# Cross-attention in seven products: other signs, a denominator taken from T3, and a new order around half 1

## The chip, the cores and the metric

The kernel runs on one NeuronCore of a Trainium2 chip. The metric is the device time of one execution in microseconds (us); lower is better. Engines are named as in the profile: PE (TensorE matmul), PEld (its weight loads), DVE (VectorE), ACT (ScalarE), POOL (GpSimd), SP (SyncE, which here only issues DMAs).

## What is computed

```python
q = jnp.einsum('bcn,dc->bnd', x1, Wq) + bq
k = jnp.einsum('bcn,dc->bdn', x2, Wk) + bk[:, None]
v = jnp.einsum('bcn,dc->bdn', x2, Wv) + bv[:, None]
attn = jax.nn.softmax(jnp.einsum('bnd,bdm->bnm', q, k), axis=2)
return jnp.einsum('bcm,bnm->bcn', v, attn) + x1
```

All is float32. There are 8 batches (b0 to b7 below), C = 512 channels, D = 64, N = 1024 positions. The softmax runs over m (the keys).

## The kernel before

**Two big products per batch.** The kernel first forms Y = x2 · softmax' (512 x 1024 by 1024 x 1024, the softmax without its denominator) and then out = Wv · Y + bv + x1. Each of the two is cut into quarters "11", "12", "21", "22" and done with seven products instead of eight (Winograd's form), numbered 1, 2, 6, 7, 5, 3, 4 in the order in which a table (MULT, L408) and the code run them. A product takes a left sum (of x2's quarters: S1 to S4) and a right sum (of the exponentials' quarters: T1 to T4). "y1" below is product 1 of Y, "o6" is product 6 of out.

In the exponentials, h is the half of the queries n (tile e[h]) and g the half of the keys m. The quarters are named in open_t: "11" is e[0] at g 0, "21" is e[0] at g 1, "12" is e[1] at g 0, "22" is e[1] at g 1. So "12" and "22" together are all of query half 1, and their sum over m is that half's denominator. Before the change the sums are T1 = 12 - 11, T2 = T1 - 22, T3 = 22 - 12 (written over "12"), T4 = 21 + T2; and S1 = 21 + 22, S2 = 11 - S1, S3 = 11 - 21, S4 = 12 + S2.

**A product inside a product.** Most Y products (multiply_seeded, L595) are once more cut into quarters and done by seven small products of 128 x 256 (inner_product, L513; four matmul records each). Their own left sums (left_stream, L478, four DVE operations of 128x256) and right sums (right_stream, L491, one DVE operation of 128x1024 and two of 128x512) are called "left" and "right" of a product below; the tiles are eI1, eI2, eI5, eI7, eI3, eI4 (right) and aI (left). Inside one product ACT copies the chain bank four times and one bank to an SBUF tile v; complete (L624) lets DVE add v at the end. A dictionary of hooks puts further ACT work between these steps.

**Order.** The program is written out by hand (manual_schedule), each engine runs its instructions in the order of the code, and waits are put between engines where tiles depend on each other. A tile with one buffer under a tag is only written again once its last reader is done, a DMA that stores it included. period (L868) is one batch: y1, y2, y6, the scores of the next batch n for half 0 (and the queries of the one after, nn), y5, y7, y3, scores of n for half 1 (and keys of nn), y4, then o1, o6, o2, o5 and o7 woven, o3, o4. b0 has its own branch; b1 to b5 have n and nn (the code's `five`); b6 has no nn; b7 has neither.

**What the change touches.**

- Softmax of a half: fold (L242) and fold_halves (L256) make a running maximum or sum over key tiles on DVE, highest (L260) and total (L266) end it with an all-reduce over partitions on POOL (L264, L269). Then invert (L275) takes the reciprocal and writes a row to DRAM, spread (L281) reads it back over 128 partitions; shares is both. lower (L296) subtracts the maximum on DVE, exponential (L306) is ACT's exp. Half 0's sum is made by accumulating DMAs (add_tile, L723).
- Denominator of half 1: three folds of e[1] on DVE, at the start of the batch's own period, and total(s, 1).
- T sums: sum_e (L349) is T1 and T2 on DVE. sum_t3 (L338) negates "12" on ACT and adds "22" by an accumulating DMA that POOL issues. copy_t4 (ACT) and add_t4 (POOL's DMA) make T4.
- S1 of the next batch: begin_s1 (L152) loads a quarter by SP, end_s1 (L157) adds another by POOL's DMA; negate and add_11 make S2 and S3 from it.
- Results: evict_o (L670) takes a quarter of out from PSUM; for "11", "22" and "12" POOL's DMA adds x1 and SP stores the tile (L720, L721). The tile of "11" has the tag u1, that of "12" the tag r. u1 is also a tile of product 5's right sums, r is also the tile v of product 5.
- PSUM banks: the scores' second tile (b1 to b5) or third (b6) goes to bank "c", which evict_y(s, "11") reads before.

```python
            weave(folds(s, 1, "sum", ALU.add), left_stream(s, 7, s.a["S3"], "yT4"))
            total(s, 1)
            invert(s, 0)
            complete_2 = multiply_seeded(
                s, 2, "y22", {5: lambda: copy_u1(s, 0), 4: lambda: copy_u1(s, 1)}
            )
            sum_t3(s, 0)
            sum_t3(s, 2)
            complete_2()
            evict_y(s, "11")
            copy_t4(s)
            add_t4(s)
```

Of the kernel before, what the change touches and what calls it, by code (L numbers as in the profile page):

```python
# [15 lines left out]
def kernel(  # L16
# [84 lines left out]
    def left_sums(a, *ks):  # L101

        for k in ks:
            if k == "S3":
                nc.vector.tensor_tensor(a["21"], a["11"], a["21"], ALU.subtract)
                a["S3"] = a["21"]
            elif k == "S4":
                nc.vector.tensor_tensor(a[k], a["12"], a["S2"], ALU.add)
            else:
                x, y, op = {"S1": ("21", "22", ALU.add), "S2": ("11", "S1", ALU.subtract)}[k]  # L110
                nc.vector.tensor_tensor(a[k], a[x], a[y], op)
# [13 lines left out]
    class Batch:  # L125
        def __init__(self, b):
            self.b = b
            self.a, self.e, self.t, self.y, self.o = {}, {}, {}, {}, {}
            self.mx, self.top, self.den, self.few, self.rden, self.row = {}, {}, {}, {}, {}, {}
            self.tmp, self.bank = {}, {}  # L130
            self.inner = {}

# [18 lines left out]

    def begin_s1(s):  # L152
# [113 lines left out]
    def total(s, h):  # L266
        fold_halves(s, h, ALU.add)
        s.den[h] = sb.tile([P, H], F32, tag="den", name=f"den_{s.b}_{h}", bufs=2)
# [45 lines left out]
    def right_sums(t, k):  # L314

        x, y = {"T1": ("12", "11"), "T2": ("T1", "22"), "T3": ("22", "12"), "T4": ("21", "T2")}[k]
        nc.vector.tensor_tensor(t[k], t[x], t[y], ALU.add if k == "T4" else ALU.subtract)
# [8 lines left out]
    def copy_t4(s):  # L326

        s.t["T4"] = t4 = sb.tile([P, MH, H], F32, tag="eT4", name=f"eT4_{s.b}")
        for i in (0, 2):
            nc.scalar.copy(t4[:, i : i + 2, :], s.t["21"][:, i : i + 2, :])  # L330
# [7 lines left out]
    def sum_t3(s, i):  # L338

        t3 = s.t["T3"][:, i : i + 2, :]  # L340
        nc.scalar.mul(t3, t3, -1.0)
        nc.gpsimd.dma_start(t3, s.t["22"][:, i : i + 2, :], accum_op=ALU.add)

    def copy_u1(s, j):
        if j == 0:
            s.tmp[1] = sb.tile([P, 2, H], F32, tag="yT1", name=f"uy1_{s.b}")
        nc.scalar.copy(s.tmp[1][:, j, :], s.bank["a", j])
# [51 lines left out]

    def iter_t4(s):  # L400
        sum_y(s, "T4")
        yield
# [126 lines left out]
    def inner_parts(s, i):  # L529

        ks = ("third", "chain") if i in (2, 7) else ("chain", "third")
        of = {k: ps_s.tile([P, 2, H], F32, tag="sc", name=f"ps_i{i}{k}_{s.b}")[:, 0, left] for k in ks}
        return of["chain"], of["third"]
# [61 lines left out]
    def multiply_seeded(s, i, v_tag, hooks={}, bank=None):  # L595
# [11 lines left out]
        v = sb.tile([P, 2, H], F32, tag=v_tag, name=f"v{i}_{s.b}")[:, 0, left]  # L607
# [16 lines left out]
        def complete():  # L624
            b = b1.rearrange("p (a n) -> p a n", a=2)
            nc.vector.tensor_tensor(b, b, v.unsqueeze(1).to_broadcast([P, 2, H // 2]), ALU.add)
# [6 lines left out]
    def copy_7(s, j):  # L633
        if j == 0:
            s.tmp[7] = sb.tile([P, 2, H], F32, tag="u1", name=f"uy7_{s.b}")
        nc.scalar.copy(s.tmp[7][:, j, :], s.bank["c", j])
# [15 lines left out]
    def evict_y(s, k):  # L652

        bank, add = RESULT[k]
        if k == "22" or s.b == B - 1 and k == "21":
            bank, add = "a", 6
        s.y[k] = y = sb.tile([P, 2, H], F32, tag=f"y{k}", name=f"y{k}_{s.b}")
        for j in range(2):
            nc.vector.tensor_tensor(y[:, j, :], s.bank[bank, j], s.tmp[add][:, j, :], ALU.add)
# [10 lines left out]
    def evict_o(s, k):  # L670
# [37 lines left out]
        if add is None:  # L708
            o = sb.tile([P, 2, H], F32, tag="u1" if k == "11" else "r", name=f"r{k}_{s.b}")
            for j in range(2):  # L710
                nc.scalar.activation(o[:, j, :], s.bank[bank, j], AF.Identity, bias=bias(j))  # L711
        else:
# [6 lines left out]
        if k != "21":  # L719
            nc.gpsimd.dma_start(o, block(s, k, x1), accum_op=ALU.add)  # L720
        nc.sync.dma_start(block(s, k, out), o)  # L721
# [146 lines left out]
    def period(s, n, nn, nnn):  # L868
# [25 lines left out]
        def scores_0():  # L894
            then = scores_and(n, 0, 1 if nn else 2, "c", next_queries if nn else nothing)
            if nn is None:
                first(6, (1,))
            if s.b:
                for i in range(1, MH):
                    fold(n, 0, i, "max", ALU.max)  # L900
                highest(n, 0)
            return then
# [4 lines left out]

        def first_sum():
# [3 lines left out]
        open_t(s)  # L912
        if s.b == 0:
# [6 lines left out]
            s.a["S4"] = sb.tile([P, MH, C // 2], F32, tag="aS4", name=f"aS4_{s.b}")  # L920
            nc.scalar.copy(s.a["S4"], s.a["S2"])
            nc.gpsimd.dma_start(s.a["S4"], x2T[s.b, 0, 1], accum_op=ALU.add)
# [12 lines left out]
            for i in range(1, MH):  # L935
# [29 lines left out]
        else:  # L965
            complete_1 = multiply_seeded(s, 1, "y11")
            sum_e(s, "T1", "T2")
            complete_1()
            sums_5 = left_stream(s, 5, s.a["S1"], "i2"), right_stream(s, 5, s.t["T1"], "y21", "u1")
            if n:  # L970
                weave(folds(s, 1, "sum", ALU.add), left_stream(s, 7, s.a["S3"], "yT4"))
                total(s, 1)
                invert(s, 0)
            else:
                weave(folds(s, 1, "sum", ALU.add), left_stream(s, 7, s.a["S3"], "yT4"))
                weave(*sums_5)
            complete_2 = multiply_seeded(
                s, 2, "y22", {5: lambda: copy_u1(s, 0), 4: lambda: copy_u1(s, 1)}
            )
            sum_t3(s, 0)  # L980
            sum_t3(s, 2)
            if n is None:
                total(s, 1)
            complete_2()
            evict_y(s, "11")
            copy_t4(s)
            add_t4(s)
            first(6, (0,) if n and nn is None else range(2))
            if n:
                weave(*sums_5)  # L990
            if n:
                sum_a(s, "S4")
                evict_q = scores_0()
                spread(s, 0)
                shares(s, 1)
            if n:
                weave(right_stream(s, 7, s.t["T3"], "yT1", "yT2"), left_stream(s, 3, s.a["S4"], "aI3"))
            else:
                sum_a(s, "S4")
                weave(right_stream(s, 7, s.t["T3"], "yT1", "yT2"), left_stream(s, 3, s.a["S4"], "aI3"))  # L1000
                invert(s, 0)
                spread(s, 0)
# [4 lines left out]
            if n is None:  # L1007
                shares(s, 1)
            if n:
                weave(right_stream(s, 3, s.t["22"], "eT1"), lowers(n, 0, 0, 1))  # L1010
# [8 lines left out]
            if n:  # L1019
                lower(n, 0, 1)  # L1020
            complete_3 = multiply_seeded(s, 3, "r", hooks, "c")
# [6 lines left out]
            if n:  # L1028
                for i in range(2, MH):
                    lower(n, 0, i)  # L1030
            complete_3()
            evict_t3(s)
        if n:
            if s.b:
                load_a(n, "11")
            begin_s1(n)
# [15 lines left out]
            end_s1(n)  # L1052
            if nn:
                next_keys()
        if late and n:
            weave(left_stream(s, 4, s.a["22"], "a12"), right_stream(s, 4, s.t["T4"], "eT2"))
        if late:
            scale_y(s, "11", "T3", "22")
# [3 lines left out]
        if five:  # L1062
            weave(folds(n, 1, "max", ALU.max))
# [8 lines left out]
        if five:  # L1072
            highest(n, 1)
        complete_4()
        if late and n:
            negate(n, "S3")
# [10 lines left out]
        scale_y(s, "21")  # L1087
        if s.b == 0:
# [4 lines left out]
        if five:  # L1093
            weave(iter_t4(s), right_stream(s, "o7", s.y["T3"], "eT1"))
# [4 lines left out]
        if late and n and not five:  # L1099
            weave(folds(n, 1, "max", ALU.max), right_stream(s, "o7", s.y["T3"], "eT1"))  # L1100
# [11 lines left out]
        second(6)  # L1112
        if n:
# [8 lines left out]
        evict_o(s, "11")  # L1122
        if n:
            if not five:
                add_tile(n, 0, 3)
            if late:
                inner_left(n, 1, n.a["11"], "i2")
        if late:
            complete_7, rest = multiply_57(s)
        else:  # L1130
# [4 lines left out]
        if n:  # L1135
            for i in range(MH) if s.b else (2,):
# [5 lines left out]
        if n:  # L1142
            negate(n, "S2")
            add_11(n, "S2")
        evict_o(s, "22")
# [3 lines left out]
        if n:  # L1149
            weave(  # L1150
                right_stream(n, 1, n.e[0][:, 0], "yT1", "yT2"), left_stream(n, 2, n.a["12"], "aS4")
# [4 lines left out]
            evict_o(s, "12")  # L1156
# [46 lines left out]
```

## Time and profile before

| what | value |
|---|---|
| median of 3 runs | 677.41 us (676.89 to 677.58) |
| the profiled execution's own time | 677.15 us |
| its span in the profile | 675.4 us |
| granted TensorE clock, mean | 0.998 |
| moved by DMA | 134.26 MB, 199 GB/s |

The span runs from the first to the last instruction of the program in the profile; 1.75 us of the execution lie around it. A row of the timeline gives start, duration, engine, line, operation and tiles, how many instructions of the kind follow each other (x4), and in brackets how long the engine idled before it and what ended that. A matmul on PE is pipelined: its record's duration is longer than the step from one to the next, so steps are read from the starts.

### The profile page before, as it was taken

How to read it: one execution, taken by the hardware profiler on the slowest of the kernel's cores; microseconds unless marked ns; L12 is line 12 of the kernel's file. 1: busy time of each engine (PE TensorE's matmuls, PEld its weight loads, DVE VectorE, ACT ScalarE, POOL GpSimd, SP SyncE). 2: the span in 40 equal slices, each digit the busy share in tenths (PEclk: the TensorE clock that was granted, in tenths of full speed). 3: DMA queues.
4: the chain of work that ended last, by engine and by line, in shares of the span. 5: the costliest groups of instructions: out<-in, count | busy, mean ns of one | idle time of the engine just before them, and what ended most of it. 6: DMA issues, size and time to landing. Idle time of an engine off the chain costs nothing.

```text
span 675.4 us, 7565 instructions
## 1 busy us (share of the span) xinstructions
PE 666.4 (99%) x2510; PEld 413.1 (61%) x2510; DVE 612.5 (91%) x811; ACT 358.5 (53%) x619; POOL 218.2 (32%) x188
## 2 busy tenths in 40 slices
PE   8999999999999999999999999999999999999996
PEld 5334754766556665657656486574855757566853
DVE  1999999999999889998999979999899989999984
ACT  3755456366465464654745647445565456565321
POOL 0126206260344411642134411445122460153400
PEclk9999999999999999999999999999999999999999
DMA  9678798958997959969599695996969968489412
GB/s 304 272 207 278 190 264 152 247 116 245 249 212 192 196 172 301 173 184 249 152 276 190 179 267 151 240 214 175 270 108 222 218 136 231 94 154 251 80 42 98
DMA packets 51638, 134.26 MB, mean 199 GB/s; under 512 B 5648, under 2 KB 7952, under 8 KB 51600
## 3 DMA queue, kind: packets, MB, share of 16 engines
q0 software_dynamic: 23328, 57.75, 47.9%
q1 hardware_dynamic: 27984, 75.64, 31.0%
q10 hardware_dynamic: 288, 0.39, 0.2%
q8 instruction: 20, 0.33, 0.2%
q14 instruction: 18, 0.15, 0.1%
HBM read 88.35 MB, written 16.81 MB: 156 GB/s over the span
## 4 chain that ended last, share of the span: by engine, by line
PE 87%; DVE 7%; DMA 3%; POOL 1%; issue 1%; SPq 1%; ACT 0%; DVEq 0%; POOLq 0%
PE ps_yc L518 10%; PE ps_ya L437 7%; PE ps_oa L559 6%; PE ps_ya L518 5%; PE ps_oa L437 5%; PE ps_s L228 5%; PE ps_o L437 4%; PE ps_oc L437 4%; PE ps_o L457 4%; PE ps_q L181 4%; PE ps_k L181 3%; PE ps_i4chain L518 3%; PE ps_i5chain L518 3%; PE ps_i7chain L518 3%; PE ps_i3chain L518 3%; PE ps_i1chain L518 2%
## 5 line engine op out<-in xcount | busy, mean ns | idle before, releaser
L269 POOL PARTITION_ALL_REDUCE den<-sum x16 | 52.5, 3283 | 72.7 <-DVE few L277 52.6
L724 POOL DMA_DIRECT2D sum<-e x21 | 27.9, 1328 | 145.7 <-ACT sum L729 71.6
L299 DVE TENSOR_TENSOR e<-e,top 128x1024 f32<-128x1024 f32 x60 | 70.6, 1218 | 0.4 <-POOL top L264 0.4
L308 ACT ACTIVATE e<-e 128x1024 f32<-128x1024 f32 x60 | 61.5, 1055 | 8.4 <-DVE e L299 7.8
L237 ACT COPY e<-ps_s 128x1024 f32<-128x1024 f32 x46 | 45.7, 1031 | 8.3 <-PE ps_s L228 8.3
L437 PE MATMUL ps_ya<-eT,aS 128*128 128x512 f32 x112 | 49.5, 593 | 0.0
L228 PE MATMUL ps_s<-q,k 64*128 64x512 f32 x188 | 47.5, 609 | 0.8 <-ACT q L751 0.8
L264 POOL PARTITION_ALL_REDUCE top<-max x16 | 31.0, 1940 | 52.1 <-DVE few L277 20.4
L248 DVE TENSOR_TENSOR max<-max,e 128x1024 f32<-128x1024 f32 x30 | 36.7, 1225 | 2.5
L437 PEld LDWEIGHTS ps_ya<-eT,aS 128*128 128x128 f32 x112 | 21.2, 190 | 24.1 <-issue 23.5
L284 POOL DMA_DIRECT2D den<-row x16 | 9.0, 561 | 78.0 <-DMA row<-few 75.0
L228 PEld LDWEIGHTS ps_s<-q,k 64*128 64x128 f32 x188 | 16.8, 186 | 24.8 <-issue 16.3
L720 POOL DMA_DIRECT2D r<-in_x_dram x14 | 29.3, 2090 | 2.9 <-ACT r L711 2.9
L648 DVE TENSOR_TENSOR y<-y,den 128x1024 f32<-128x1024 f32 x24 | 29.3, 1220 | 0.2
L437 PE MATMUL ps_o<-y,w 128*128 128x512 f32 x64 | 28.8, 592 | 0.0
L457 PE MATMUL ps_o<-y,w 128*128 128x512 f32 x64 | 28.8, 592 | 0.0
L437 PE MATMUL ps_oa<-yT,w_S 128*128 128x512 f32 x64 | 28.8, 592 | 0.0
L437 PE MATMUL ps_oc<-yT,w 128*128 128x512 f32 x64 | 28.8, 592 | 0.0
L611 ACT COPY ps_yc<-ps_i7chain 128x256 f32<-128x256 f32 x32 | 11.4, 357 | 30.3 <-PE ps_i7chain L518 22.3
L611 ACT COPY ps_ya<-ps_i5chain 128x256 f32<-128x256 f32 x32 | 11.4, 358 | 29.9 <-PE ps_i5chain L518 25.7
L485 DVE TENSOR_TENSOR aI<-a,aI 128x256 f32<-128x256 f32 x60 | 26.0, 433 | 1.0
L611 ACT COPY ps_ya<-ps_i1chain 128x256 f32<-128x256 f32 x28 | 10.0, 357 | 30.6 <-PE ps_i1chain L518 27.0
(257 smaller groups left out, 1734.8 us busy)
## 6 DMA issues: line engine op xcount, KB each, us to landing
x_in_x_dram<-in_x_dram SPq DMA_DIRECT2D x60, 512.0 KB, 9.3
a<-in_x2T_dram SPq DMA_DIRECT2D x32, 512.0 KB, 9.5
sum<-e POOLq DMA_DIRECT2D x21, 512.0 KB, 7.5
eT<-eT POOLq DMA_DIRECT2D x16, 512.0 KB, 10.9
aS<-in_x2T_dram POOLq DMA_DIRECT2D x15, 512.0 KB, 7.4
uo<-in_x_dram POOLq DMA_DIRECT2D x14, 512.0 KB, 9.6
r<-in_x_dram POOLq DMA_DIRECT2D x14, 512.0 KB, 11.5
out_dram<-r SPq DMA_DIRECT2D x14, 512.0 KB, 3.4
```

Of the source, the lines that this page charges most:

```text
L181: nc.tensor.matmul(ps[r, :], w_sb[:, c, :], s.x[:, c, ts(h, H)], start=(c == 0), stop=(c == CT - 1),)
L228: nc.tensor.matmul(ps[g], s.k[r, ts(i, P)], s.q[r, ts(h, H)], start=True, stop=True)
L237: nc.scalar.copy(e[:, :, i, :], whole)
L248: nc.vector.tensor_tensor(f, e[:, :, 0, :] if i == 1 else f, e[:, :, i, :], op)
L269: nc.gpsimd.partition_all_reduce(s.den[h], s.mx[h][:, 0, :], P, ReduceOp.add)
L299: nc.vector.tensor_tensor(e, e, top, ALU.subtract)
L308: nc.scalar.activation(e, e, AF.Exp)
L437: nc.tensor.matmul(ps[:, n], left[ka][:, k, ts(j, P)], right[kb][:, k, n], start=opens and k == 0, stop=i in (2, 3, 4) and k == n_k - 1, s ...
L457: nc.tensor.matmul(ps, w["11"][:, k, ts(j, P)], s.y["11"][:, k, :], start=k == 0, stop=False, skip_group_check=True)
L518: nc.tensor.matmul(ps, s.inner[i][ka][:, k, :], s.inner[i, "t"][kb][:, k, :], start=opens and k == 0, stop=z in (2, 3, 4) and k == n_k - 1 ...
L559: nc.tensor.matmul(ps[:, n], w[ka][:, k, ts(j, P)], s.y[kb][:, k, n], start=False, stop=i == 3 and k == 1, skip_group_check=True,)
L611: nc.scalar.copy(out, of)
```

## The change

Signs: S1 becomes 21 - 22, S4 becomes 12 - S2, T2 becomes T1 + 22, T3 becomes 22 + 12, T4 becomes T2 - 21, and product 7 enters with the other sign (copy_7, evict_y). T3 is then the sum of half 1's two key halves, so its four tiles of 128x512 need one more addition of 128x1024 (sum_1) before fold_halves.

Order, for b1 to b5 as the current batch: the maximum of n's half 1 is folded earlier (between scale_y calls), lower and exponential of that half go before and into o2 and o5/o7, S2 is made there too; T1 and T3 of n are formed at the end of the current period instead of in n's own; x1 is added to and stored for quarter "12" ("22" and "12" after b0 and b6) in n's period. In the own period of b2 to b5, product 5's sums come where the three folds were, total_1 comes between y2 and complete_2, product 7's left sums and S4 after evict_y "11", and product 7's right sums among the folds of n's half 0. In b6 product 4's sums come ahead of the last two lowers. S1's first part is an ACT operation on a loaded quarter instead of a load.

The diff also has branches for a flag `six`; it is set to False for every batch and nowhere changed, so they never run and are left out here.

```diff
             elif k == "S4":
-                nc.vector.tensor_tensor(a[k], a["12"], a["S2"], ALU.add)
+                nc.vector.tensor_tensor(a[k], a["12"], a["S2"], ALU.subtract)
...
     def begin_s1(s):
 
         s.a["S1"] = sb.tile([P, MH, C // 2], F32, tag="aS1", name=f"aS1_{s.b}")
-        nc.sync.dma_start(s.a["S1"], x2T[s.b, 1, 0])
+        nc.scalar.mul(s.a["S1"], s.a["22"], -1.0)
 
     def end_s1(s):
 
-        nc.gpsimd.dma_start(s.a["S1"], x2T[s.b, 1, 1], accum_op=ALU.add)
+        nc.gpsimd.dma_start(s.a["S1"], x2T[s.b, 1, 0], accum_op=ALU.add)
...
+    def sum_1(s):
+
+        t = s.t["T3"]
+        s.mx[1] = sb.tile([P, 2, H], F32, tag="fold", name=f"sum_{s.b}_1", bufs=2)
+        nc.vector.tensor_tensor(s.mx[1], t[:, 0:2, :], t[:, 2:4, :], ALU.add)
+        fold_halves(s, 1, ALU.add)
+
+    def total_1(s):
+        sum_1(s)
+        reduce_total(s, 1)
...
     def sum_t3(s, i):
 
         t3 = s.t["T3"][:, i : i + 2, :]
-        nc.scalar.mul(t3, t3, -1.0)
         nc.gpsimd.dma_start(t3, s.t["22"][:, i : i + 2, :], accum_op=ALU.add)
...
             elif s.b:
+                weave(folds(n, 0, "max", ALU.max), right_stream(s, 7, s.t["T3"], "yT1", "yT2"))
                 highest(n, 0)
...
+        def while_11(j):
+            if five:
+                exponential(n, 1, j)
+            elif j:
+                early_s2()
...
             more_keys(2, 3)
             load_x(nn, x1)
             parts_6(s, 2)
-            for i in range(1, MH):
-                fold(s, 1, i, "sum", ALU.add)
-            total(s, 1)
             sum_e(s, "T3")
+            total_1(s)
             weave(right_stream(s, 5, s.t["T1"], "y21", "u5"))
...
+            early = s.b > 1 and n is not None
+            sum_e(s, *(("T2",) if early else ("T1", "T2")))
+            if s.b > 1:
+                complete_1()
...
+            if not early:
+                sum_t3(s, 0)
+                sum_t3(s, 2)
+            for leave in s.leave:
+                leave()
+            if n and not early:
                 invert(s, 0)
...
                 weave(*sums_5)
+            if n is None:
+                weave(left_stream(s, 7, s.a["S3"], "yT4"))
             complete_2 = multiply_seeded(
...
+            if s.b > 1:
+                total_1(s)
             complete_2()
             evict_y(s, "11")
+            if early or n is None:
+                invert(s, 0)
+            if n is None:
+                spread(s, 0)
...
+                copy_t4(s)
+                add_t4(s)
+                first(6, (0,) if n and nn is None else range(2))
             if n:
+                weave(left_stream(s, 7, s.a["S3"], "yT4"))
...
             complete_5()
-            if n is None:
-                shares(s, 1)
+            shares(s, 1)
             if n:
-                weave(right_stream(s, 3, s.t["22"], "eT1"), lowers(n, 0, 0, 1))
+                weave(right_stream(s, 3, s.t["22"], "eT1"), left_stream(s, 3, s.a["S4"], "aI3"))
+                lower(n, 0, 0)
...
+            sums_4 = (left_stream(s, 4, s.a["22"], "a12"), right_stream(s, 4, s.t["T4"], "eT2"))
+            if five:
                 for i in range(2, MH):
                     lower(n, 0, i)
+            elif n:
+                weave(*sums_4)
             complete_3()
             evict_t3(s)
...
+        if five:
+            weave(*sums_4)
+            scale_y(s, "11")
+            fold(n, 1, 1, "max", ALU.max)
+            scale_y(s, "T3")
+            fold(n, 1, 2, "max", ALU.max)
+        elif late:
+            scale_y(s, "11", "T3")
+            if n:
+                lower(n, 0, 2)
+                lower(n, 0, 3)
+            scale_y(s, "22")
...
         if five:
-            weave(iter_t4(s), right_stream(s, "o7", s.y["T3"], "eT1"))
+            lower(n, 1, 0)
+            lower(n, 1, 1)
+            inner_right(s, "o7", s.y["T3"], "eT1")
+            lower(n, 1, 2)
...
-        evict_o(s, "11")
+        evict_o(s, "11", while_11 if nn else None)
...
+        if five:
+            open_t(n)
+            sum_e(n, "T1")
+            sum_t3(n, 0)
+            sum_t3(n, 2)
+        if five:
+            leave()
...
-            evict_o(s, "12")
+            last = evict_o(s, "12")
+            n.leave = [last] if five else [leave, last]
```

More of the change, by code (lines that the diff above doesn't have):

```diff
@@ L606, in multiply_seeded @@
         chain, third = inner_parts(s, i)
-        v = sb.tile([P, 2, H], F32, tag=v_tag, name=f"v{i}_{s.b}")[:, 0, left]
+        if v_tag == "top" or s.b == B - 1 and v_tag == "r":
+            v = sb.tile([P, H], F32, tag="top", name=f"v{i}_{s.b}", bufs=2)[:, left]
+        else:
+            v = sb.tile([P, 2, H], F32, tag=v_tag, name=f"v{i}_{s.b}")[:, 0, left]
         def step(z, ps, opens, out=None, of=None):
@@ L919, in period @@
             fold(s, 0, 3, "sum", ALU.add)
[L920 to L922 removed]
+            copied_s4(s)
+            add_s4(s)
             copy_t4(s)
@@ L965, in period @@
         else:
[L966 to L972, printed above, removed]
+            complete_1 = multiply_seeded(s, 1, "y11", {4: lambda: copied_s4(s)} if s.six else {})
+            if s.b == 1:
+                complete_1()
```

162 lines of the change are left out of this document (104 added, 58 removed).

## The prediction, made before the changed kernel was run

> **What bounds the kernel now.** I read the page's first part, then the waits of PE, then the busy time by stretches cut where y1 of a batch starts, then the timeline of PE where the stretches differ.
>
> ```profile
> PE 666.4 (99%) x2510; PEld 413.1 (61%) x2510; DVE 612.5 (91%) x811; ACT 358.5 (53%) x619; POOL 218.2 (32%) x188
> ```
> ```profile
> PE ps_s L228 <- ACT q L751: 0.8, 1, 0.8
> ```
> ```profile
> 281.30:362.88 81.58, 81.58 (x311) 51.51 (x310) 75.50 (x101) 45.67 (x79) 28.22 (x26) 1.00 0.86 212
> ...
> 444.46:526.04 81.58, 81.58 (x311) 51.44 (x310) 75.28 (x101) 45.68 (x79) 28.17 (x26) 1.00 0.85 197
> 526.04:602.24 76.20, 75.54 (x280) 49.15 (x279) 73.86 (x99) 43.53 (x76) 28.50 (x26) 1.00 0.73 164
> ```
>
> PE is busy in all of b3 and b5 (rows 1 and 2; columns: length, then PE, PEld, DVE, ACT, POOL), and both have the same length to the hundredth. A stretch that repeats exactly with PE full is PE's own work: 81.58 us, in which DVE has 6 us to spare. The longest wait of PE anywhere is 0.8 us, in the head, where the diff changes nothing but signs. The diff changes no matmul. So it can only win what PE loses elsewhere, and it can lose without such a bound. I look for stalls shorter than a record, which "busy" hides.
>
> ```profile
> 467.21 3.58 PE ps_q L181 x16
> ...
> 492.76 3.58 PE ps_k L181 x16
> ...
> 575.32 0.86 PE ps_yc L518 x4
> ```
> ```profile
> 555.20 1.03 PE L518 MATMUL ps_i7chain<-e,a 128*128 128x256 f32 x4
> 556.36 1.10 PE L518 MATMUL ps_i7third<-eI7yT,aI 128*128 128x256 f32 x4
> 557.29 1.10 PE L518 MATMUL ps_i7chain<-eI7yT,aI 128*128 128x256 f32 x4
> ...
> 571.46 1.13 PE L518 MATMUL ps_i4chain<-eT,a 128*128 128x256 f32 x4
> 572.95 1.10 PE L518 MATMUL ps_i4third<-eI4eT,aI 128*128 128x256 f32 x4 [0.36 <-DVE eI4eT L500]
> 574.22 1.10 PE L518 MATMUL ps_i4chain<-eI4eT,aI 128*128 128x256 f32 x4 [0.17 <-DVE aI L485]
> ```
>
> b6 has no queries and keys to project: 81.58 - 2 x 3.58 = 74.42, but it takes 76.20, so it **loses 1.78**. A small product steps every 0.86 (third row of the chain). In y7 two steps take 2.09 instead of 1.72: 0.37 lost. In y4 two take 2.76: 1.04 lost, of which 0.1 is usual after a change of kind (b0's first step below shows it), so 0.94. The other 0.47 lies at the scores and in steps not shown.
>
> ```profile
> 61.87 1.13 PE L518 MATMUL ps_i5chain<-eT,aS 128*128 128x256 f32 x4
> 62.84 1.03 PE L518 MATMUL ps_i5third<-eI5y,aI 128*128 128x256 f32 x4
> ...
> 68.44 1.03 PE L518 MATMUL ps_i7chain<-e,a 128*128 128x256 f32 x4
> ```
> ```profile
> 307.57 1.13 PE L518 MATMUL ps_i5chain<-eT,aS 128*128 128x256 f32 x4
> ...
> 313.71 1.03 PE L518 MATMUL ps_i7chain<-e,a 128*128 128x256 f32 x4
> ```
> ```profile
> 627.37 1.03 PE L518 MATMUL ps_i7chain<-e,a 128*128 128x256 f32 x4
> 628.46 1.10 PE L518 MATMUL ps_i7third<-eI7yT,aI 128*128 128x256 f32 x4
> ```
>
> y5 takes 6.57 in b0 and 6.14 in b3: **0.43 lost**. y7 of b7 loses 0.23 in one step. All that is to be had is 1.78 + 0.43 + 0.23 = 2.44; with steps of b7 that I don't list I allow 2.8.
>
> **The change part by part.** *Signs* swap add and subtract at the same sizes: nothing.
>
> *Denominator of half 1.* Three folds go, sum_1 comes: two DVE operations of 1.2 fewer per batch, 2.4 us. ACT loses two negations of 1.06 and gains one (S1), SP loses one load.
>
> ```profile
> L248 DVE TENSOR_TENSOR sum<-sum,e 128x1024 f32<-128x1024 f32 x18 | 21.9, 1214 | 0.2
> ...
> L341 ACT ACTIVATE e<-e 128x1024 f32<-128x1024 f32 x14 | 14.9, 1062 | 9.3 <-DVE sum L248 9.3
> ```
> ```profile
> e<-e POOLq DMA_DIRECT2D x14, 512.0 KB, 5.6
> ```
>
> In b1 to b5 that lies beside a full PE: worth **0** there. In return DVE now waits at sum_1 for the DMA that makes T3 (median 5.6 to landing).
>
> *b0.* The folds stand just ahead of product 5's right sums, for which PE is late; 2.4 us earlier they are ready before 62.84: **-0.43**.
>
> *b2 to b5, between y2 and the scores.* Here is the new danger: evict_y "11" must free bank "c" before the scores' second tile.
>
> ```profile
> 291.24 1.21 DVE L248 TENSOR_TENSOR sum<-e 128x1024 f32<-128x1024 f32 x1
> ...
> 296.11 0.69 DVE L258 TENSOR_TENSOR sum<-sum 128x512 f32<-128x512 f32 x1
> ...
> 298.57 0.84 DVE L485 TENSOR_TENSOR aI<-aS 128x256 f32<-128x256 f32 x1
> ...
> 302.68 1.21 DVE L108 TENSOR_TENSOR aS<-a,aS 128x1024 f32<-128x1024 f32 x1
> ```
> ```profile
> 301.31 1.02 PE L228 MATMUL ps_sc<-q,k 64*128 64x512 f32 x4
> ```
> ```profile
> L721 SPq DMA_DIRECT2D out_dram<-r x2: 372/384/395, 284.0 to 294.5; - x2
> ...
> DMA to landing us min/median/max: 2.9/4.9/10.1
> ```
>
> Before, evict_y "11" ends where the third row starts, at 298.57. Out of its way go the folds with product 7's left sums (291.24 to 296.11, 4.9) and an inversion (0.1); in come product 5's sums (298.57 to 302.68, 4.1) and sum_1 (1.2): +0.3. T1 moves ahead into the tail and T2 stays; their sum is the same, and the lowers that end the tail in one block are spread over the o products, so DVE comes to y1 as before. One wait is new. Product 5's second right sum writes tag u1, which SP's store of quarter "11" still reads: issued at 284.0, landed 10.1 later, at 294.1 (last fence). DVE gets there at about 293.3 (291.24 + 0.84 + 1.2): 0.8 wait. Together 299.7, against 301.31: **1.6 us of room, cost 0**. Behind DVE's wait stand sum_1, complete_2 and evict_y, and PE waits for the last. Bounds of the wait: 0 (the store meets an empty queue, 2.9) and 0.8 + 2 x 2.9 (both of T3's transfers, of the same size, go ahead of it). I take 0.8, the row's own landing: T3's two transfers take the place of x1 for "12", which moves back, so the number of POOL's transfers around the store grows by one only.
>
> The Trainium skill's page "DMA: Bandwidth & Descriptors", section "Queues, rings and completion order", says that each DMA engine takes turns between the queues that have work, a packet at a time. By that the store shares evenly with POOL's transfers however many are queued, and the sum stays as it is; 10.1 beside 2.9 shows that it got less than an even share here. With first come, first served it would be rival A.
>
> *Queues that steps are moved past.* T3's two transfers (POOL) now precede the x1 of "12", whose store must be done before product 5's tile v (tag r) is written, in its third step; by the landings above it is, by some us. S1's negation stands before ACT's key bias, where ACT waits for PE's projection anyway. In b1 to b5 the exps of half 1 go between ACT's copies of o2 and of o5, where ACT waits for PE: at most 0.1. The reduce of half 1's maximum still comes after an accumulation into half 0's sum. All 0.
>
> *b6, y7.* DVE waited for T3's transfer, and PE for DVE:
>
> ```profile
> 554.98 1.23 DVE L500 TENSOR_TENSOR eI7yT<-e 128x1024 f32<-128x1024 f32 x1 [1.75 <-DMA e<-e]
> ```
>
> T3 is now asked for in b5's tail, and eI7 stands among the folds: **-0.4**. Nothing is late next.
>
> *b6, y4.* eI4 comes behind two lowers, complete_3 and evict_t3:
>
> ```profile
> 565.98 1.29 DVE L659 TENSOR_TENSOR y<-ps_ya,uy 128x512 f32<-128x512 f32 x2
> 567.19 2.35 DVE L299 TENSOR_TENSOR e<-e,top 128x1024 f32<-128x1024 f32 x2
> 569.46 0.69 DVE L626 TENSOR_TENSOR ps_yc<-ps_yc,v 128x512 f32<-128x512 f32 x1
> ...
> 571.25 0.42 DVE L485 TENSOR_TENSOR aI<-a 128x256 f32<-128x256 f32 x1
> ...
> 574.93 1.22 DVE L648 TENSOR_TENSOR y<-y,den 128x1024 f32<-128x1024 f32 x1
> ...
> 577.20 1.22 DVE L648 TENSOR_TENSOR y<-y,den 128x1024 f32<-128x1024 f32 x1
> ```
>
> Now product 4's sums start straight after evict_y, at 567.2 instead of 571.25: -0.94. But the lowers go behind evict_t3 and two scalings, and the exp of tile 2 is hooked into y4's third step, on ACT, ahead of the copy that y4's last step needs. I count on from 567.2 less 1.0 (PE is earlier by the 0.4 above and 0.2 below, and join_67 no longer follows a late lower): 3.7 for product 4's sums (571.25 to 574.93), 1.8 for complete_3 and evict_t3 (569.46 to 571.25), 2.3 for two scalings (574.93 to 577.20), 1.15 for the lower: 575.1; exp (1.06) and a copy: 576.5. PE wants its last step six steps after 570.9 (571.46 less 0.6), at 576.1: +0.4. Bounds: 0, and 1.4 if DVE is 1 us later. Net **-0.55**.
>
> *b6, scores.* Two negations less on ACT ahead of the first copies of the scores bring 0.3 of the 0.47; bank "c" comes 0.3 later and keeps some. **-0.2**. *b7, y7*: its right sums come 2 us earlier, **-0.23**.
>
> The sum: 0.43 + 0.4 + 0.55 + 0.2 + 0.23 = 1.8, with the steps not listed **1.9 us**. The own time 677.15 (span 675.4 and 1.75 around it) less 1.9 is 675.25; the median of the runs, 677.41, is 0.26 higher, which makes 675.5. I write **675.4**.
>
> **The rivals.** *A. Slower, through bank "c"*: the store of "11" lands behind one or both of T3's transfers, in each of b2 to b5. Room 1.6, wait beyond the forecast 2.9 to 5.8: with the lower, 1.3 a batch, 5.2 in all, less 1.9: 680.6 on the median's scale (677.41 + 3.3 = 680.7). It decides from a landing 1.6 us later than before. For it: that store took 10.1 while POOL's transfers ran. Against: it took turns with them, and their number is nearly the same. *B. T3 not there*: DVE finds sum_1's input not landed, 1 us past the room in b2 to b5; the folds waited for nothing, so the saved 2.4 us turn into a wait: 4.0 - 1.9 gives 679.5. For it: e<-e made DVE wait before. Against: the transfers start before y1 and sum_1 comes after y2's sums. *C. Given back*: in b6 ACT's queue in y4 costs 1.4 instead of 0.4, and in b7 T4's transfers, now behind the read-back of a denominator row in POOL's queue, reach eI4 up to 0.7 late: 1.9 - 1.7 gives 677.2. For it: both margins are under 1 us by my count.
>
> **How the numbers follow.** A measurement of this kernel can tell about 0.2% (1.35 us) from no change. Chances: forecast 0.55, C 0.18, A 0.17, B 0.10. Of the forecast 0.53 lies beyond 0.2%; so faster 0.53, same 0.20 (C and the rest), slower 0.27 (A and B). Low end: all 2.8 gone, 674.4. High end: past B, 680.0, leaving out A and little else.
>
> **What would show it.** Right: b2 to b5 keep 81.58 with PE full; b6 is near 75.0; y5 of b0 takes 6.14; eI7 of b6 waits for no DMA. Wrong: a stretch over 81.6 among b2 to b5 with the scores' second tile (ps_sc) waiting for DVE's y (A if DVE idled inside product 5's right sums, B if before the sum); in b6 a step of y4 waiting for ACT behind an exp (C); eI4 of b7 waiting for T4 (C). The whole prediction falls if a matmul of b1 to b5 reads a tile that my walk along DVE's order puts too early.

## The result and the profile after

The changed kernel takes 684.65 us (median of 4 runs, 683.65 to 685.61) beside 677.25 us before in the same session (4 runs, 676.89 to 677.58). The ratio is 1.0109, 95% interval 1.0092 to 1.0127: **slower by 1.1%**, where 675.4 us and "faster" were forecast. The profiled execution took 685.01 us with a span of 683.0 us and a mean granted clock of 0.993, beside 677.15, 675.4 and 0.998 before. I look for the 7.6 us of span.

The first part of the page after, engine by engine:

```profile
PE 669.7 (98%) x2510; PEld 415.8 (61%) x2510; DVE 595.3 (87%) x795; ACT 353.1 (52%) x612; POOL 219.5 (32%) x188
```

DVE does what the diff says: 17 us less work, 16 instructions fewer. PE has the same 2510 instructions and is busy 3.3 us longer: the same work went slower somewhere. Next, the busy time by stretches, from one y2 to the next (columns: length, PE, PEld, DVE, ACT, POOL, granted clock, DMA share, GB/s). Before, the stretches of b1, b6 and b7 (b2 to b5 took 81.58 each):

```profile
124.07:205.77 81.70, 81.70 (x312) 51.89 (x311) 77.59 (x103) 45.65 (x79) 30.75 (x25) 1.00 0.86 213
...
532.09:608.28 76.19, 75.53 (x280) 49.15 (x278) 72.78 (x99) 43.53 (x76) 26.26 (x24) 1.00 0.74 167
608.28:675.40 67.12, 61.57 (x223) 41.61 (x221) 54.97 (x79) 21.09 (x46) 12.35 (x12) 0.98 0.45 117
```

After, b1, b2, b3, b6 and b7:

```profile
124.53:214.13 89.60, 84.19 (x312) 53.11 (x311) 76.45 (x101) 44.80 (x78) 32.56 (x28) 0.96 0.82 198
214.13:295.71 81.58, 81.58 (x312) 51.51 (x311) 74.37 (x99) 44.86 (x78) 28.26 (x25) 1.00 0.80 197
295.71:378.29 82.58, 82.44 (x312) 52.19 (x311) 72.61 (x99) 45.15 (x78) 28.23 (x25) 1.00 0.85 207
...
541.45:616.64 75.19, 75.14 (x279) 49.36 (x278) 68.83 (x96) 42.75 (x75) 24.07 (x22) 1.00 0.70 155
616.64:683.00 66.36, 61.48 (x223) 41.62 (x221) 53.90 (x78) 19.30 (x44) 15.84 (x14) 0.98 0.49 122
```

Ahead of b1's y2 the kernel is 0.46 later (124.53 against 124.07). **b1 is longer by 7.90**, at a lower clock; b3 is longer by 1.00; b2 (and b4 and b5, whose rows read alike) keep 81.58 to the hundredth; b6 is shorter by 1.00 and b7 by 0.76, of which 0.62 lies behind the last matmul. 0.46 + 7.90 + 1.00 - 1.00 - 0.76 = 7.60. So the gain forecast for b6 is there, and one batch that I had put down at nothing loses nearly eight times as much. The 0.46 is there already at the ps_k records of PE in b0 that start at 44.10 instead of 43.65. In r6_all_mended below, whose program is the same up to there, they start at 43.66, so the 0.46 need not come from the change.

In b1 the waits of PE name one place, and the chain of waits around it says what ended last:

```profile
PE ps_i5chain L544 <- ACT ps_ya L640: 5.4, 1, 5.4
```
```profile
130.16 14.33 DMA r<-in_x_dram
...
144.54 8.53 DMA out_dram<-r
...
153.88 2.08 PE ps_i5chain L544 x4
```

Read from below: PE's fifth step of product 5 waits for a chain copy of ACT; ACT stands at the copy into v (next fence); v has the tag r, which SP is still storing as quarter 12; the store was issued when x1 had been added, 14.33 us after POOL asked for it. ACT's own timeline, after, says it in one row:

```profile
153.18 0.37 ACT L640 COPY v<-ps_i5third 128x256 f32<-128x256 f32 x1 [6.85 <-DMA out_dram<-r]
```

And the stop costs more than its length. The stretches around it, after (the first number behind POOL's is the granted clock):

```profile
148.40:154.00 5.60, 0.19 (x2) 0.12 (x1) 1.43 (x3) 0.82 (x3) 2.22 (x2) 0.81 1.04 377
154.00:156.00 2.00, 2.00 (x5) 1.64 (x6) 0.00 (x0) 1.12 (x3) 0.00 (x0) 0.50 1.01 408
156.00:158.00 2.00, 2.00 (x6) 1.55 (x6) 0.00 (x0) 0.65 (x2) 0.00 (x0) 0.50 1.06 277
158.00:160.00 2.00, 2.00 (x10) 1.70 (x9) 1.66 (x3) 0.05 (x1) 0.55 (x1) 0.84 0.90 223
```

PE works at half the clock from 153.88 to about 158.65, so it loses about 2.3 more: 5.6 + 2.3 = 7.9, all of b1.

Why was the store so late? POOL's timeline, before and then after:

```profile
117.16 1.20 POOL L720 DMA_DIRECT2D r<-in_x_dram  x1 [0.52 <-ACT r L711]
...
141.16 1.77 POOL L342 DMA_DIRECT2D e<-e  x2 [0.26 <-PE ps_s L228]
142.28 2.40 POOL L336 DMA_DIRECT2D eT<-eT  x2
```
```profile
128.34 1.75 POOL L367 DMA_DIRECT2D e<-e  x2 [0.32 <-issue]
129.44 1.88 POOL L755 DMA_DIRECT2D uo<-in_x_dram  x1
130.16 2.38 POOL L755 DMA_DIRECT2D r<-in_x_dram  x1
...
132.02 2.90 POOL L362 DMA_DIRECT2D eT<-eT  x2
```

Before, POOL asked for x1 of quarter 12 at 117.16, and T3's and T4's transfers (e<-e, eT<-eT) at 141 and 142, when b0's quarters had long left. After, T3's stand at 128, x1 of the two quarters behind them at 129 and 130, and T4's at 132. From asking to landing x1 of 12 took no longer than before (14.33 us; before 14.46, up to the store's issue at 131.62); it was asked for 13.0 us later. The store itself also took longer, in the list of DMA issues at 131.6 before and at 144.5 after (last number: us to landing):

```profile
out_dram<-r SPq DMA_DIRECT2D x1, 512.0 KB, 2.9
```
```profile
out_dram<-r SPq DMA_DIRECT2D x1, 512.0 KB, 8.5
```

b3's 1.00 is another wait. After, DVE in b3, at product 5's second right sum:

```profile
304.90 0.69 DVE L531 TENSOR_TENSOR eI5u<-eI5y,eT 128x512 f32<-128x512 f32 x1 [3.43 <-DMA out_dram<-r]
```

That is the tag u1, the store of quarter 11, with evict_y and the scores' second tile behind it: rival A's wait, in one batch.

### The profile page after: what moved, and what is told of

It reads as the page before. It is cut to its first block, busy times and chain, and to the rows that moved or that the text cites. A ratio compares the mean times of both kernels' runs of the same rounds, so it can differ in the third digit from the quotient of the medians.

```text
span 683.0 us, 7520 instructions
## 1 busy us (share of the span) xinstructions
PE 669.7 (98%) x2510; PEld 415.8 (61%) x2510; DVE 595.3 (87%) x795; ACT 353.1 (52%) x612; POOL 219.5 (32%) x188
## 4 chain that ended last, share of the span: by engine, by line
PE 80%; DMA 8%; DVE 7%; issue 2%; POOL 1%; SPq 1%; ACT 0%; DVEq 0%; POOLq 0%; ACTq 0%
PE ps_yc L544 10%; PE ps_ya L463 6%; PE ps_oa L585 6%; PE ps_ya L544 6%; PE ps_s L238 5%; PE ps_oa L463 4%; PE ps_oc L463 4%; PE ps_o L483 4%; PE ps_o L463 4%; PE ps_i5chain L544 3%; PE ps_q L191 3%; DMA out_dram<-r 3%; PE ps_i4chain L544 3%; PE ps_i7chain L544 3%; PE ps_i3chain L544 3%; PE ps_k L191 3%
## 5 line engine op out<-in xcount | busy, mean ns | idle before, releaser
L274 POOL PARTITION_ALL_REDUCE top<-max x16 | 32.6, 2040 | 60.4 <-DVE max L268 41.8
L677 DVE TENSOR_TENSOR y<-y,den 128x1024 f32<-128x1024 f32 x24 | 30.9, 1303 | 0.2
L655 DVE TENSOR_TENSOR ps_ya<-ps_ya,v 128x512 f32<-128x512 f32 x16 | 11.1, 692 | 22.6 <-ACT ps_ya L640 22.6
L755 POOL DMA_DIRECT2D r<-in_x_dram x14 | 27.2, 1942 | 2.3 <-ACT r L743 2.3
```

## The experiments

Theory R: b1's stop is the store of 12 that holds tag r, and the half clock behind it. Rival L: b1 is an accident, and the loss lies in waits of b2 to b5. Rival Q: the two transfers of T3 merely crowd the queues, and the tag is where it happens to show. Ten kernels ran; all medians, each beside runs of the kernel before on the same chip:

| kernel | us | ratio to before (95%) |
|---|---|---|
| changed kernel | 684.65 | 1.0109 (1.0092 to 1.0127) |
| r1_b0_leave_now | 682.27 | 1.0069 (1.0041 to 1.0097) |
| r2_own_v5 | 677.72 | 1.0006 (0.9985 to 1.0026) |
| r3_swap | 682.18 | 1.0063 (1.0043 to 1.0082) |
| r4_idle (one profiled run) | 706.84 | - |
| r5_own_v5_u1 | 675.71 | 0.9977 (0.9968 to 0.9986) |
| r6_all_mended | 675.29 | 0.9973 (0.9961 to 0.9984) |
| r7_b0_leave_u1 | 678.10 | 1.0011 (1.0002 to 1.0020) |
| r8_b6_order_back | 675.11 | 0.9969 (0.9958 to 0.9979) |
| r9_t4_later | 677.95 | 1.0008 (0.9999 to 1.0017) |
| r10_order_only | 676.16 | 0.9980 (0.9971 to 0.9989) |

**r2_own_v5** gives product 5's v in b1 a tile of its own and changes no order.

```diff
-        if v_tag == "top" or s.b == B - 1 and v_tag == "r":
+        if s.b == 1 and i == 5:
+            v = sb.tile([P, H // 2], F32, tag="v51", name=f"v{i}_{s.b}")
+        elif v_tag == "top" or s.b == B - 1 and v_tag == "r":
```

> The stores of b0 stay late, but product 5's tile v in b1 gets a place of its own (1 KB per partition) instead of the tag r. Theory R: the store of quarter 12 still lands at about 153 us, ACT no longer waits for it, b1 takes 81.6 and the time is 676.7. Rival Q: unchanged within 1 us, 684. Rival L: unchanged.

Measured: 677.72, 7 us less. ACT in b1:

```profile
146.88 0.37 ACT L642 COPY v<-ps_i5third 128x256 f32<-128x256 f32 x1 [0.45 <-PE ps_i5third L544]
```

The copy waits for PE now, as it should, 6.3 us earlier than after; the clock is 1.0. The transfers are all still there in the same order, and the store of 12, issued at 144.74, still took 8.7 us, so crowding alone (Q) doesn't make the stop. L falls too: one tag in one batch is nearly all of b1's loss, whose stretch goes from 89.60 to 82.71. Left over were 1.0 in b3 and, in this kernel, 0.9 at b1's product 3. One of its ten executions took 683.13 us; it was not profiled, and why stays open.

**r1_b0_leave_now** lets b0 add x1 to quarters 22 and 12 and store them in its own tail.

```diff
-        if five:
+        if five or s.b == 0:
             leave()
...
             n.leave = [last] if five else [leave, last]
+            if s.b == 0:
+                last()
+                n.leave = []
```

> The x1 additions and stores of quarters 22 and 12 of b0 are issued in b0's tail again, nothing else is undone. Theory R (product 5's tile v in b1 waits for the store of quarter 12, which stands behind T3's transfers; PE stops 5.4 to 6.0 us and then runs at half clock for 4.8 us, 2.0 us more): b1 takes 81.6, the time is 684.65 - 8.0 = 676.7. Rival L (b1's stop is an accident of one execution, the loss lies in DVE's waits in b2 to b5): 683 to 685. Rival Q (the stop comes from T3's and T4's transfers crowding b1, whatever the order of the two stores): most of the 8 us stays, 681 or more.

Measured: 682.27. That is where rival Q was put (681 or more), but not by Q's stop: the one at product 5 is gone, and b1 stops at the scores instead. DVE and then PE of this kernel:

```profile
134.73 0.18 DVE L301 RECIPROCAL few<-few 128x4 f32<-128x4 f32 x1 [4.38 <-DMA few<-den]
...
138.01 0.69 DVE L531 TENSOR_TENSOR eI5u<-eI5y,eT 128x512 f32<-128x512 f32 x1 [1.30 <-DMA out_dram<-r]
```
```profile
141.23 1.29 PE L238 MATMUL ps_sc<-q,k 64*128 64x512 f32 x3 [2.80 <-DVE y L691]
```

The two x1 transfers now stand ahead of the 2 KB of denominators (few<-den) and the store of 11 behind POOL's transfers: 4.38 + 1.30 of DVE's waiting reach PE as 2.80. Moving the work earlier moved the loss.

**r7_b0_leave_u1** adds to r1 that product 5's second right sums use aI3 instead of u1, which takes the 1.30 away and leaves the 4.38.

> r1_b0_leave_now (b0 leaves quarters 22 and 12 in its own tail) with product 5's second right sums in aI3 instead of u1; v of product 5 keeps tag r. r1 lost 5.3 us at b1's scores and about 1 in b3. Theory W: both were the wait for the store of quarter 11; both go, time 682.3 - 6.2 = 676.1. Theory C: b1 stops somewhere else, time above 680.

Measured: 678.10, 4.2 less than r1, not the 6.2 that I gave theory W. Its DVE row:

```profile
134.50 0.18 DVE L301 RECIPROCAL few<-few 128x4 f32<-128x4 f32 x1 [3.99 <-DMA few<-den]
```

So r1's stop was two waits in a row, and I had named only the second. The row of denominators is a third transfer that a moved x1 can hold up.

**r3_swap** lets 12 leave ahead of 22, so that one transfer fewer stands before its x1.

```diff
-            n.leave = [last] if five else [leave, last]
+            n.leave = [last] if five else [last, leave]
```

> In b1 quarter 12's addition and store go ahead of quarter 22's; both stay behind T3's transfers. Theory R: the store that the tag r waits for lands one transfer of 512 KB earlier (2.6 us), PE stops about 3.0 us instead of 5.6: 682.0 if the clock falls after a stop of 3 us as it did after 5.6, 680.0 if it doesn't. Rival Q: unchanged, 684. Rival L: unchanged.

Measured: 682.18. PE at the same place:

```profile
152.30 1.13 PE L544 MATMUL ps_i5chain<-eI5y,aI 128*128 128x256 f32 x4 [3.50 <-ACT ps_ya L640]
```

One place in POOL's queue is worth 1.9 us of the stop (5.41 to 3.50), and the clock stayed at 1.00 behind it. That holds for the profiled execution, 681.34 us. The other five took 680.36 to 683.11 at a mean clock of 0.996 to 0.998, in four of them under the 0.998 that is the lowest of before, so the clock probably fell in some of them; no trace of them shows where.

**r9_t4_later** moves T4's two transfers in b1 behind total_1 in POOL's queue; every tile keeps its tag.

```diff
                 copy_t4(s)
-                add_t4(s)
+                if s.b != 1:
+                    add_t4(s)
...
                 if s.b == 1:
                     total_1(s)
+                    add_t4(s)
```

> The changed kernel with one step moved: in b1 alone POOL issues T4's two transfers behind total_1, about 14 us later than in the changed kernel, so that they aren't under way while SP stores quarter 12. All tiles keep their tags. In the kernel before that store took 2.9 us with no other transfer under way; in the changed kernel it took 8.5 us beside T4's transfers and was issued about 13 us later, behind x1, which stands behind T3 in POOL's queue. Theory S (both count: late by the order, and stretched by T4): the store lands about 3 us after 144.5, PE's stop at product 5 shrinks from 5.4 to about 0.5 to 1.0, the clock stays, time 677.5 to 678. Theory O (the order alone, the store takes 8.5 whatever runs beside it): stop and half clock stay, 684.6.

Measured: 677.95. The store's landing in the list of issues, and PE's timeline, both of this kernel:

```profile
out_dram<-r SPq DMA_DIRECT2D x1, 512.0 KB, 4.2
```
```profile
150.09 1.13 PE L544 MATMUL ps_i5chain<-eI5y,aI 128*128 128x256 f32 x4 [1.09 <-ACT ps_ya L640]
```

x1 landed as late as in the changed kernel (SP issued the store at 145.04, there at 144.54), yet the store took 4.2 instead of 8.5. Theory S holds: the order made the store late and T4's transfers stretched it. Rival Q is right to that extent.

**r5_own_v5_u1** is r2 with product 5's second right sums in aI3.

```diff
-                right_stream(s, 5, s.t["T1"], "u5" if s.six else "y21", "u1"),
+                right_stream(s, 5, s.t["T1"], "y21", "aI3" if n else "u1"),
```

> The changed kernel with two tiles taken off the stores: product 5's tile v of b1 has a buffer of its own (as in r2_own_v5), and product 5's second right sums in b1 to b5 go to aI3, which no store reads, in place of u1. Theory W (what is left over in b3 is rival A's wait: the right sum waits for the store of quarter 11, and bank c for evict_y behind it): the 1.0 us of b3 goes, b3 takes 81.58, DVE waits for no store at eI5u, time 677.7 - 1.0 = 676.7. Theory C (the loss in b3 comes from the crowd of transfers, and the tag only says where it shows): another wait of PE of about 1 us in b3, time 677.7. Both: about 0.9 us at b1's product 3 stays.

Measured: 675.71, 2.0 less than r2, twice what theory W gave. b3 takes 81.58; its DVE waits for no store at the second right sum:

```profile
294.14 0.68 DVE L533 TENSOR_TENSOR eI5aI<-eT,eI5aI 128x512 f32<-128x512 f32 x1
```

The 0.9 at b1's product 3 went as well, which I had not aimed at. In r2 DVE had stood 2.48 there for half 1's denominators. In r2 it had also waited 2.28 for the store at b1's second right sum, ahead of sum_1; without that wait POOL's all-reduce of the sum starts at 140.49 instead of 143.12, and the denominators are there when DVE wants them.

**r6_all_mended** adds to r5 that b0's copy of the queries stands behind product 5's third chain copy, and that b1's reciprocal of half 1 goes behind product 3's right sums.

```diff
-            if five:
-                return evict
-            evict()
+            return evict
...
-            scores_0()
+            evict_q = scores_0()
...
-                complete_5 = multiply_seeded(s, 5, "r")
+                complete_5 = multiply_seeded(s, 5, "r", {6: evict_q})
```

> r5_own_v5_u1 and two moves more. In b0 the copy of the queries is hooked into product 5 of Y behind its third chain copy, as b1 to b5 have it, where it stood ahead of product 5. In b1 the reciprocal of half 1's denominator goes behind product 3's right sums and the lower instead of ahead of them. Theory A0 (b0's 0.43 in y5 is ACT's copy of the queries, 1.39 us, not DVE's folds): y5 of b0 takes 6.14 instead of 6.57. Theory D0 (it is DVE, as I predicted): 6.57 stays. The second move: if the 0.9 us at b1's product 3 is DVE waiting 2.48 us for the row of denominators, it goes. Together 676.7 - 0.43 - 0.9 = 675.4; with D0 675.8; with C 676.4 to 676.8. Before is 677.3 to 677.7.

Measured: 675.29. PE in b0's y5, in the changed kernel and then in this one:

```profile
62.32 1.13 PE L544 MATMUL ps_i5chain<-eT,aS 128*128 128x256 f32 x4
...
68.90 0.81 PE L544 MATMUL ps_i7chain<-e,a 128*128 128x256 f32 x3
```
```profile
61.87 1.13 PE L544 MATMUL ps_i5chain<-eT,aS 128*128 128x256 f32 x4
...
68.02 1.03 PE L544 MATMUL ps_i7chain<-e,a 128*128 128x256 f32 x4
```

6.58 becomes 6.15: the 0.43 of b0 is real, and it was ACT's. In the changed kernel ACT shows it:

```profile
62.43 1.39 ACT L208 ACTIVATE q<-ps_q,bqk_sb 64x512 f32<-64x512 f32 x2 [2.27 <-PE ps_q L191]
63.85 0.36 ACT L640 COPY ps_ya<-ps_i5chain 128x256 f32<-128x256 f32 x1
```

The first chain copy could start only at 63.85, behind the queries, while PE's second step had begun at 63.28. The spans of r5 and r6 differ by 0.3, so the second move adds nothing that shows.

**r8_b6_order_back** is r6 with b6's product 4 sums where they stood before the change.

> r6_all_mended with b6's product 4 sums put back where they stood before the change: behind the two lowers, complete_3 and evict_t3, ahead of the scalings. My prediction put 0.55 us on this move (0.94 won at the third and fourth steps of y4, 0.4 given back at its last step). If that holds, b6's y4 loses 0.94 in those two steps again, the last step's wait goes, and the time is 0.55 above r6_all_mended's span. If DVE's order in b6 is worth nothing, the two spans agree within 0.2 us.

Measured: 675.11, span 673.1 against 673.3: no difference. PE in b6's y4 in this kernel, then in r6:

```profile
570.43 1.13 PE L544 MATMUL ps_i4chain<-eT,a 128*128 128x256 f32 x4
571.72 1.10 PE L544 MATMUL ps_i4third<-eI4eT,aI 128*128 128x256 f32 x4 [0.16 <-DVE eI4eT L526]
572.99 1.10 PE L544 MATMUL ps_i4chain<-eI4eT,aI 128*128 128x256 f32 x4 [0.17 <-DVE aI L511]
...
577.38 1.02 PE L483 MATMUL ps_o<-y,w 128*128 128x512 f32 x2
```
```profile
570.21 1.13 PE L544 MATMUL ps_i4chain<-eT,a 128*128 128x256 f32 x4
571.39 1.13 PE L544 MATMUL ps_i4third<-eI4eT,aI 128*128 128x256 f32 x4
572.36 1.03 PE L544 MATMUL ps_i4chain<-eI4eT,aI 128*128 128x256 f32 x4
...
577.08 1.45 PE L483 MATMUL ps_o<-y,w 128*128 128x512 f32 x3
```

y4 takes 6.95 with the old order and 6.87 with the new one. The new order wins 0.41 in two steps (2.56 to 2.15) and loses 0.33 of it in the steps behind, at ACT's exps.

**r10_order_only** mends b1 without a new tile: r9's move, r3's swap, r5's aI3 and r6's queries.

> r9_t4_later with quarter 12 leaving ahead of 22 (as r3_swap), product 5's second right sums in aI3 instead of u1 (as r5_own_v5_u1) and b0's copy of the queries behind product 5's third chain copy (as r6_all_mended). No tile is added: tile v of product 5 keeps tag r. Theory S: x1 of 12 lands about 2.6 us earlier, at 142, its store by 145, ahead of the copy into v at about 147: no stop in b1, and the time of r6_all_mended, 675.3. Theory O: the store lands at about 150.5, a stop of 3 us, 678 or more.

Measured: 676.16, 0.9 more than r6. The store of 12 and PE:

```profile
out_dram<-r SPq DMA_DIRECT2D x1, 512.0 KB, 6.4
```
```profile
148.63 1.13 PE L544 MATMUL ps_i5chain<-eI5y,aI 128*128 128x256 f32 x4 [0.68 <-ACT ps_ya L640]
```

It was issued at 141.4, as expected, but x1 of 22 now ran beside it, and it landed 2.8 later than I had put it. Order alone brings most of the gain; b1 still takes 82.52, where with its own tile it takes 81.58 (r6).

**r4_idle** measures the clock by itself: on r1, ACT makes 9, 12, 15 and 18 copies more in product 5 of b2 to b5, each 128x256, so that PE stops for growing times.

```diff
+            def idle():
+                scr = sb.tile([P, H // 2], F32, tag="scr", name=f"scr_{s.b}")
+                for _ in range(3 * s.b + 3):
+                    nc.scalar.copy(scr, s.t["T1"][:, 0, left])
```

> As r1, and in product 5 of b2, b3, b4, b5 ACT does 9, 12, 15 and 18 needless copies of 128x256 ahead of the copy that PE waits for, so that PE stops about 1.9, 2.9, 3.9 and 4.9 us. It asks only when the granted clock falls. If no stop of this size costs clock: 676.7 + 13.6 = 690.3. If each costs 2.05 us more, as b1's did: 698.5. If a threshold lies between: in between, and the clock by stretches shows after which stop.

Measured: 706.84. PE's first record behind two of the stops, and the stretches that follow two (clock third from the end):

```profile
239.64 1.13 PE L544 MATMUL ps_i5chain<-eI5y,aI 128*128 128x256 f32 x4 [2.27 <-ACT ps_ya L640]
...
325.06 2.07 PE L544 MATMUL ps_i5chain<-eI5y,aI 128*128 128x256 f32 x4 [3.58 <-ACT ps_ya L640]
```
```profile
239.70:242.00 2.30, 2.30 (x11) 2.00 (x12) 0.00 (x0) 1.86 (x4) 0.00 (x0) 1.00 1.00 403
...
325.10:327.00 1.90, 1.90 (x5) 1.54 (x6) 0.00 (x0) 1.20 (x2) 0.00 (x0) 0.50 1.02 412
```

706.84 is above every forecast: the four stops came to 16.9 us in place of 13.6, r1 itself was 5.6 slower than assumed, and b1 stopped for 5.00 at its scores.

2.27 costs its length; 3.58, 4.88 and 6.19 are each followed by a record of twice the duration and a clock of 0.50. Cut into stretches of 0.02 us, the traces show when the clock changes. It stays at half for 3.41 us after r1's 2.80 (142.54 to 145.95) and after r4's 5.00, 3.58 and 4.88, and for 6.82 or 6.83, twice that, in the changed kernel (151.83 to 158.65) and after r4's 6.19. The four falls in r4, at 143.60, 324.50, 413.25 and 502.00, lie 53, 26 and 26 times 3.413 us apart. So in r4 the clock changes on a grid of 3.41 us that runs on whatever PE does, and how much of one interval PE stands counts beside the length of the stop. In r1 2.10 us of an interval lowered the clock (of a stop of 2.80, with thin work behind it); in r4 1.80 and 1.86 us (parts of the stops of 2.27 and 6.19) did not. That r3's 3.50 kept the clock because it lay across two intervals fits this but is not shown, since its trace has no fall from which to take the grid.

The Trainium skill's page "TensorE: Matmul & The Clock Gate", section "Part 1: The HAM clock gate", says that the clock falls to half after an idle window of about 3.4 us, that this window runs freely, and that about as long a busy window brings it back. The grid in r4 agrees with that. r1's 2.10 of 3.41 us shows that an interval need not be idle throughout to lower the clock.

## Why the prediction was wrong

- **The step that failed** is "Queues that steps are moved past". It said that T3's transfers precede the x1 of "12", whose store must be done before product 5's tile v is written, and that "by the landings above it is, by some us", and it ended in "All 0". Those landings were b3's of the kernel before, where one quarter leaves in n's period. I did not walk the list in b1, where two quarters leave, T1 and T3 are not yet moved to the period before, and T3, x1 of 22, x1 of 12 and T4 are all asked for within 5 us. There x1 landed at 144.5, and the store at 153.1, beside T4's transfers that the step does not mention; ACT had stood idle for 6.85 us. x1 itself was no slower there than before; it was asked for 13.0 us later. r2 (one tile) and r9 (one order) show the wait from two sides. 5.6 of the 7.9 us is this wait.
- **The clock** had no term. A forecast with the stop at its right length would still have missed the 2.3 us at half speed.
- **b2 to b5, rival A.** The mechanism was named and priced at 1.3 a batch; it came in b3 alone, at 1.0. The store of 11, in the chain of waits after, took there what I had taken over from before:

```profile
294.26 10.52 DMA out_dram<-r
```

  10.5 us against 10.1. But it was issued 1.5 us ahead of y2 (at 295.71), where before it had been 3.3 (284.01 to 287.35), so it landed 2.3 later than before by that measure. DVE's wait was 3.43 where I took 0.8; less my 1.6 of room that leaves the 1.0 that PE lost. The room was right: in b2, b4 and b5 DVE waited 0.5 to 1.1 at the same place, and 1.85 in b3 of r9, and PE lost nothing. POOL asked for x1 of 11 13.96 us ahead of y2 in b3 (281.75), 15.91 in b2 (198.22). It asked behind accumulations into half 0's sum, and the second of these came 9.91 us after the first in b3 (258.91 to 268.82), 8.07 in b2; the first had taken 8.8 us to land in b3 and 7.5 in b2. Why it was slower there stays open.
- **Rival B** came where I had not put it: in b7 DVE stands 0.84 for T3 at sum_1, product 7's right sums come behind that, and y7 of b7 wins 0.05 instead of 0.23. DVE after, in b7:

```profile
629.99 1.23 DVE L284 TENSOR_TENSOR sum<-e 128x1024 f32<-128x1024 f32 x1 [0.84 <-DMA e<-e]
```

- **b0, -0.43**: nothing came. The size was right and the engine wrong: DVE's folds stood next to the stall, but ACT's copy of the queries ended it. r6 moved that copy and got the 0.43.
- **b6, -1.15**: 1.00 came. y7 gave 0.44 of 0.4 and the scores 0.27 of 0.2. y4 gave 0.28 (7.15 to 6.87) of 0.55, and by r8 only 0.08 of it is due to the new order of DVE; the other 0.20 came with PE and DVE being earlier.
- **Signs and the shorter sums in b1 to b5, 0**: right. DVE's saved 2 us a batch are worth nothing where PE is full, as b2, b4 and b5 show. (PE's longest wait before was 1.0 us, for a warm-up tile in the head, and not 0.8; no term rests on it.)

With the two tags out of the way the time is 675.71 (r5), 675.29 with the queries moved, against 677.69 before in that session. So about the 1.9 that I summed was there to be had, but that the size fits is in part luck: r5 has nothing of b0's 0.43, and some 0.6 of its gain lies behind the last matmul (5.48 us before, 4.85 in r5), for which I had no term and whose cause stays open. What the moved transfers held up cost 8.9 (7.9 in b1, 1.0 in b3). r6 and r8 are faster than the kernel before by 0.3%.

## What to carry to other kernels

When a step with DMAs moves, follow every transfer that is then behind it in the same queue to the tile that it frees, and to that tile's next writer, in each batch whose order differs and not only in the one that repeats; add what runs beside it to its landing time. A store that holds a small scratch tile was mended more fully here by another tile (r6) than by another order (r10). Price a stop of PE of about 3 us or more at its length and, as a second case, another 1.4 to 3.0 us for the clock. Six stops of 2.80 to 6.19 cost that here (half the time that PE worked at half clock), one of 3.50 nothing. Give a stall to the engine that released it, not to the one whose work stands beside it.

## What the hardware showed unexpectedly

- The same store of 512 KB on SP took 2.9 us with nothing of POOL's under way (before, beside two other stores of SP's), 4.2 with SP's own loads behind it (r9), 6.4 beside one x1 (r10) and 8.5 beside T4's two transfers (after). In the changed kernel, from 144.3 to 146.3, around that store's issue, POOL's queue had 101.0% of the DMA engines' time and SP's 2.1%, although the store of 22 had been asked for at 141.96. The Trainium skill's page "DMA: Bandwidth & Descriptors", section "Queues, rings and completion order", has each DMA engine take turns between queues. By an estimate from that rule the store would take twice its 2.9, 5.8; the shares above say that POOL's queue got far more than an even part here, and the measurement decides.
- A 2 KB transfer of POOL's (few<-den) took 7.5 us to land in r1 and 7.2 in r7, where x1 of 22 and 12 had been asked for ahead of it, and 2.0 in r5 and 2.2 in r6, where they come behind it. It kept DVE waiting 4.38 and 3.99 us in r1 and r7 and not at all in r5 and r6: however small, it waited for its place.
- The clock fell to 0.50 after stops of 2.80 (r1) and 3.58 (r4), not after 3.50 (r3) or 2.27 (r4). Where it fell it stayed down for 3.41 us or for twice that, and in r4 the falls lie on a grid of 3.413 us: where a stop falls on the grid counts beside its length.
